# Gate's products for two token tiles at once: 256 columns instead of 128, and turned rows kept in pairs

## The chip, the core and the metric

The kernel runs on one core of a Trainium2 chip. The metric is the device time of one execution in microseconds. Before the change it is 1980.17 us, the median of 3 runs (1979.7 to 1982.45).

## What is computed

The reference is one transformer block: cross attention whose keys and queries both come from a context, then a mixture of eight experts beside one shared expert. Cut to what matters:

```python
# x: (4, 1024, 1024); four batches, 4096 tokens in all
x = x + attention(ctx) applied to layernorm(x)     # mixes the columns of each row
xt = layernorm(x).reshape(4096, 1024)
scores = sigmoid(xt @ gate_w.T)                    # gate_w: (8, 1024)
_, sel = top_k(scores + expert_bias, 2)
shared = silu(xt @ sw1.T) * (xt @ sw3.T) @ sw2.T   # the shared expert, float32
routed = grouped_swiglu(xt[tok] * score, w1, w2, w3)   # bfloat16, two experts a token
out = x + shared.at[tok].add(routed)
```

"Gate" below is the product `xt @ gate_w.T`: eight numbers for each token.

## The kernel before, in words

The tokens lie in 32 tiles of 128 rows (`NT`). A tile has 1024 columns, which are 8 blocks of 128 (`KC`); `HALF` is 4.

The work has four stages. The first, up to about 63 us, makes the attention of the first batch. The second takes the tiles in 16 pairs (loop over `p`, L583; `g = 2 * p` is the first tile). The third is the shared expert, in 8 blocks of 512 tokens (`up`, L913, and `down_pair`, L1009; the first block's `up` is `first_up`, L191, at the end of stage two). The fourth is the routed experts, in slots of 512 tokens (loop at L1125).

A pair of tiles of stage two consists of seven products of 512 columns (`product`, L399, through `seven`, L197; the matmuls are at L129). They are a 2 by 2 product in Strassen's manner, written out in seven terms. After each product comes a step `between(k)`, k from 0 to 6 (L619), which adds other work to TensorE's queue. This order is written by hand: in this stage TensorE, GpSimd, VectorE and ScalarE execute in the order of the program text, and only SP's queue (the loads and stores) is ordered by the framework's own scheduler. While three batches remain ahead (`ahead`, pairs 0 to 11), a pair also prepares two tiles of the next batch's attention: `energies` (L317), `softmax` (L326), `scaled` (L333), and `turned` (L342), which transposes the attention rows. In the last four pairs (12 to 15) nothing lies ahead, and these are left out.

The tiles touched by the change are these. A pair's sums, `x`, are normalised on ScalarE into `xt` (`second_norm`, L426). `turn` (L432) transposes the eight blocks of `xt` on TensorE into two PSUM tiles, `pt_t`, which ScalarE copies to `xtT` (L260). SP stores `xtT` to DRAM, `xtd` (L435), for the shared expert. `gate_parts` (L438) multiplies `xtT` by the gate's weights: eight matmuls of 128 columns in four groups of 32 array columns, each over two blocks, into the PSUM tile `gp` (L443); ScalarE copies it to `gs` (L446). `gate` (L449) adds the four groups with a small matmul with `sel`, into `lg` (L450). `route` (L452), `counts`, `lists_of` (L493), `weighted` (L513) and `scatter` (L523) then choose the experts and scatter the rows on VectorE, ScalarE and GpSimd.

The transposes of all kinds and `gp` share one pool of two PSUM buffers with the tag `pt` (`ps_t`, L115). `xtT` and `gs` have two SBUF buffers each, since pool `p2` (L231) has two by default.

In pairs 1 to 11 the order on TensorE is: turn of the previous pair's first tile; product 1; its gate; product 2; turn of the second tile; product 3; energies; product 4; gate of the second tile; `lg` of the first; transposes `pt_a` of `turned`; `lg` of the second; product 5, and so on. In pairs 12 to 15 it is: product 1; turn of the first; product 2; its gate; product 3; turn of the second; product 4; its gate; both `lg`; product 5. After the loop the last pair (tiles 30 and 31) is turned and gated among the first products of the shared expert, `pu` (L720 to L732).

The shared expert loads a block's turned rows with one DMA (`block`, L152) into `xb`, in which a row of 128 partitions has the axes tile, block of columns and token. `up` uses it as the moving operand, and GpSimd makes differences of its quarters, `xs` (L1109).

Of the kernel before, what the change touches and what calls it, by code (L numbers as in the profile page):

```python
# [31 lines left out]
F32 = mybir.dt.float32  # L32
# [8 lines left out]
P = 128  # L41
B, S, D = 4, 1024, 1024
C = 512
T = B * S
NT = T // P
HID = 704
E = 8
KC = D // P
# [6 lines left out]
G = 2  # L55
SLOT = 512
NQ = SLOT // P
# [20 lines left out]
def xattn_moe_kernel(ctx: ExitStack, tc: tile.TileContext, x, ctxT, wqT, wkT, bqk, gwT, ebias,  # L78
                     w13, w2, w2t, sw13, sw2, sw2t, consts, out):
    nc = tc.nc  # L80

    dram = ctx.enter_context(tc.tile_pool(name="dram", bufs=1, space=DRAM))
# [2 lines left out]
    w2tb = dram.tile([E * TAIL, D], BF16, name="w2tb")  # L85
    xrows = nc.dram_tensor("xrows", (E * T, ROW // 2), I32, kind="Internal").ap()
    x2d = dram.tile([T, D], F32, name="x2d")
    xtd = dram.tile([NT, P, D], F32, name="xtd")

    cp = ctx.enter_context(tc.tile_pool(name="cp", bufs=1))  # L90
    con = cp.tile([P, CONSTS], F32, name="con")
# [58 lines left out]
    cps, cur = [], {}  # L150

    def block(s):  # L152
        cur["xb"] = xb = cps[1].tile([P, NQ, KC, P], F32, tag="xb", name=f"xb_{s}")
        nc.sync.dma_start(xb.rearrange("p t c k -> p t (c k)"),
                          xtd[s * NQ : (s + 1) * NQ].rearrange("t p f -> p t f"))

    def of_two(ap):

# [68 lines left out]
    with ExitStack() as a:  # L227
# [22 lines left out]
        def transposed(dsts, src, n, second=None):  # L250

            for h, dst in enumerate(dsts):
                pt = ps_t.tile([P, HALF, P], F32, tag="pt", name=f"pt_{n}_{h}")
                for j in range(HALF):
                    c = h * HALF + j
                    nc.tensor.transpose(pt[:, j, :], src[:, c * P : (c + 1) * P], ident)  # L256
                if h and second:
                    nc.vector.tensor_copy(dst, pt)
                else:
                    nc.scalar.copy(dst, pt)  # L260
# [165 lines left out]
        def second_norm(g):  # L426
# [2 lines left out]
            xts[g] = xt = p2.tile([P, D], F32, tag="xt", name=f"xt_{g}", bufs=4)  # L429
            nc.scalar.activation(xt, x2, AF.Identity, bias=nb, scale=rs)  # L430

        def turn(g):  # L432
            xtT = p2.tile([P, KC, P], F32, tag="xtT", name=f"xtT_{g}")
            transposed([xtT[:, :HALF], xtT[:, HALF:]], xts[g], f"t{g}")
            nc.sync.dma_start(xtd[g], xtT.rearrange("p c t -> p (c t)"))  # L435
            return xtT

        def gate_parts(g, xtT):  # L438

            gp = ps_t.tile([P, P], F32, tag="pt", name=f"gp_{g}")  # L440
            for r in range(2):
                for j in range(4):
                    nc.tensor.matmul(gp[32 * j : 32 * (j + 1), :], gw_sb[:, 2 * j + r, :],  # L443
                                     xtT[:, 2 * j + r, :], start=r == 0, stop=r == 1)
            gs = p2.tile([P, P], F32, tag="gs", name=f"gs_{g}")
            nc.scalar.copy(gs, gp)  # L446
            return gs

        def gate(lg, g, gs):  # L449
            nc.tensor.matmul(lg[:, g % G, :], gs, sel, start=True, stop=True)  # L450

        def route(g, lg):  # L452

# [91 lines left out]
        with tc.manual_schedule(engines=vector_scalar):  # L545
# [33 lines left out]
            ps_a.close()  # L579
            ps_m, ps_e, ps_s = psum("ps_m", 1), psum("ps_e", 1), psum("ps_s", 1)  # L580

            routing, listing, xtTs, gss = {}, {}, {}, {}
            for p in range(NT // 2):  # L583
                g = 2 * p
                b, i = divmod(g, LT)
# [25 lines left out]
                    looked(i)  # L611
                if p:
                    if ahead:
                        xtTs[g - 2] = turn(g - 2)
                    second_norm(g - 1)
                if not new:
                    softened(i)
# [1 line left out]
                def between(k):  # L619
                    if k == 0:  # L620
                        if not ahead:
                            xtTs[g - 2] = turn(g - 2)
                        elif p:
                            gss[g - 2] = gate_parts(g - 2, xtTs.pop(g - 2))
                        if new:
                            next(halves)
                        if p > 1:
                            pc_, ss, ohs = listing[g - 4]
                            listing[g - 4] = lists_of(g - 4, pc_, ohs), ss
                        if g + 2 < NT:  # L630
                            load(g + 2)
                            load(g + 3)
                        if g == NT - LT:
                            nc.sync.dma_start(sw13_sb, sw13)
                    elif k == 1:
                        if new:
                            looked(i)
                            softened(i)
                        if not ahead:
                            gss[g - 2] = gate_parts(g - 2, xtTs.pop(g - 2))  # L640
                        elif p:
                            xtTs[g - 1] = turn(g - 1)
                        if ahead:
                            scaled(b + 1, i, on_scalar=True)
                        if p > 1:
                            tois, ss = listing.pop(g - 4)
                            listing[g - 4] = tois, [weighted(g - 4, j, ss) for j in range(G)]
                        if p in (1, 3, 5, 7, 10, 13):
                            convert((1, 3, 5, 7, 10, 13).index(p))
                    elif k == 2:  # L650
                        if not ahead:
                            xtTs[g - 1] = turn(g - 1)
                        looked(i + 1)
                        softened(i + 1)
                        if g + 2 < NT:
                            norms[g + 2] = statistics(xin[g + 2], f"1_{g + 2}")
                        if g + 2 == NT:
                            two_sums.close()
                            cps.append(pool(shared, "c3"))
                            block(0)  # L660
                    elif k == 3:
                        if p:
                            gss[g - 1] = gate_parts(g - 1, xtTs.pop(g - 1))
                            lg = ps_s.tile([P, G, E], F32, tag="lg", name=f"lg_{g}")
                            gate(lg, g - 2, gss.pop(g - 2))
                        if ahead:
                            turned(b + 1, i)
                            scaled(b + 1, i + 1, on_scalar=True)
                        if p:
                            gate(lg, g - 1, gss.pop(g - 1))  # L670
                            routing[g - 2] = route(g - 2, lg)
                        if p > 1:
                            scatter(g - 4, *listing.pop(g - 4))
                        if g + 2 < NT:
                            norms[g + 3] = statistics(xin[g + 3], f"1_{g + 3}")
                    elif k == 4:
                        if ahead:
                            turned(b + 1, i + 1)
                    elif k == 5:
                        if g + 2 < NT:  # L680
                            tokens(g + 2)
                        if p:
# [35 lines left out]
            v21, v22 = sw2_sb[:, KH : 2 * KH, :512], sw2_sb[:, KH : 2 * KH, 512:]  # L718
            ups = first_up(pool(a, "e1", 1, "right"))
            g = NT - 2  # L720
            xtT = turn(g)
            second_norm(g + 1)
            pc_, ss, ohs = listing.pop(g - 2)
            tois = lists_of(g - 2, pc_, ohs)
            next(ups)
            gs = gate_parts(g, xtT)
            xtT = turn(g + 1)
            scatter(g - 2, tois, [weighted(g - 2, j, ss) for j in range(G)])
            next(ups)
            lg = bank("lg_last")[:, : G * E].rearrange("p (g e) -> p g e", g=G)  # L730
            gate(lg, g, gs)
            gate(lg, g + 1, gate_parts(g + 1, xtT))  # L732
            nc.vector.tensor_tensor(ws[0], w21, w22, ALU.add)
            mask, ss, ohs = route(g, lg)
            next(ups)
# [172 lines left out]
    with shared, tc.manual_schedule(engines=vector_scalar | {mybir.EngineType.SP}):  # L908
# [4 lines left out]
        def up(s):  # L913
# [3 lines left out]
            for f in range(NF):  # L917
                if f == 1:
                    residuals(s)
                cols = slice(f * P, (f + 1) * P)  # L920
                a = [lambda c, w=w: w[:, c, cols] for w in (w11, w12, w22, *ws, w21)]
                b = [lambda c, x=x: x[:, :, c, :]
                     for x in (xb[:, :2, :HALF], xb[:, :2, HALF:], xb[:, 2:, HALF:], *cur["xs"])]
                pa, pb, pc_ = (bank(f"p{k}_{s}_{f}")[:, :256] for k in "abc")

                one, two, five = (c1.tile([P, 256], F32, tag=k, name=f"{k}_{s}_{f}", bufs=n)
# [151 lines left out]
        for s in range(NJ):  # L1078
# [25 lines left out]
            down_pair(s, 0)  # L1104
            if s + 1 < NJ:
                xb = cur["xb"]
                cur["xs"] = xs = [sx.tile([P, 2, HALF, P], F32, tag=f"xs{i}", name=f"xs{i}_{s}")
                                  for i in range(4)]
                differences(nc.gpsimd, xs[:3], xb[:, :2, :HALF], xb[:, 2:, :HALF], xb[:, :2, HALF:],  # L1109
                            xb[:, 2:, HALF:], xs[3], False)  # L1110
# [167 lines left out]
```

## Time and profile before

| what | us |
|---|---|
| median of 3 runs (range) | 1980.17 (1979.7 to 1982.45) |
| the profiled execution | 1977.36 |
| its span in the profile | 1975.6 |
| TensorE (PE) busy | 1940.2 |
| gate's matmuls (`gp<-xtT,gw_sb`), 512 records | 20.6 |
| transposes of `turn` (`pt_t`), 256 records | 33.5 |
| `lg` matmuls, 60 and 4 records | 10.6 for the 60 |
| granted TensorE clock | 0.997 |

The profile is of one execution; times in it count from the start of its span. PE is TensorE's matmuls and PEld its weight loads, which run beside them; DVE is VectorE, ACT ScalarE, POOL GpSimd, SP the queue of loads and stores. [...] The record of a matmul is longer than the distance to the next one, because matmuls are pipelined; distances between starts tell what TensorE spends. "a<-b,c" reads: tile a is written from b and c. An arrow after idle time names what ended it.

### The profile page before, as it was taken

The page shows a single profiled execution, that of the slowest core. Times are in us where ns is not written, and L with a number is a line of the kernel's source. Part 1 is how long each engine was busy: PE and PEld are TensorE (multiplying, and loading weights), DVE is VectorE, ACT ScalarE, POOL GpSimd, SP SyncE. Part 2 cuts the span into 40 slices and gives each one's busy share as a digit, 9 for nine tenths or more (in the row PEclk, how much of TensorE's full clock was granted, in tenths as well). Part 3 has the DMA queues.
Part 4 walks back from the last instruction along what each step waited for, and adds up shares of the span by engine and source line. Part 5 has one row for each costly group of instructions (what it writes and reads, how often), then busy time and mean ns, then how long its engine had stood idle before and what let it go on. Part 6 is the DMA issues. An engine that isn't in the chain of part 4 may idle for free.

```text
span 1975.6 us, 23759 instructions
## 1 busy us (share of the span) xinstructions
PE 1940.2 (98%) x8736; PEld 1157.9 (59%) x8851; DVE 809.3 (41%) x1981; ACT 514.4 (26%) x900; POOL 651.7 (33%) x598
## 2 busy tenths in 40 slices
PE   8999999999999999999999999999999999999997
PEld 5555655655444447676676758584845555446554
DVE  5456556555865324413232323223243333223343
ACT  3344454355434101010110101010102233223232
POOL 0424433543642140302222232213014454335454
PEclk9999999999999999999999999999999999999999
DMA  3277486447685216297776868586465598649995
GB/s 124 85 173 196 141 226 165 138 143 195 244 228 204 96 64 152 78 231 208 209 199 167 198 196 212 143 207 181 114 284 108 111 312 277 139 137 325 345 353 93
DMA packets 229394, 365.51 MB, mean 185 GB/s; under 512 B 114336, under 2 KB 170144, under 8 KB 222496
## 3 DMA queue, kind: packets, MB, share of 16 engines
q0 software_dynamic: 43024, 172.78, 33.0%
q1 hardware_dynamic: 186256, 191.21, 32.1%
q8 instruction: 71, 1.16, 0.2%
q14 instruction: 43, 0.35, 0.1%
HBM read 289.19 MB, written 174.59 MB: 235 GB/s over the span
## 4 chain that ended last, share of the span: by engine, by line
PE 91%; DMA 3%; DVE 2%; issue 1%; SPq 1%; POOL 1%; ACT 0%; POOLq 0%; DVEq 0%; ACTq 0%
PE pa L129 21%; PE bank L129 15%; PE pc L129 11%; PE bank L1150 7%; PE qa L129 6%; PE pb L129 5%; PE pu L129 4%; PE pq L308 3%; PE qc L129 3%; PE pe L320 3%; PE pt_c L129 2%; DMA xh<-xgt 2%; PE pt_a L256 1%; PE qb L129 1%; PE pt_t L256 1%; PE pt_x L256 1%
## 5 line engine op out<-in xcount | busy, mean ns | idle before, releaser
L129 PE MATMUL bank<-xTb,w 128*128 128x0 bf16 x2024 | 310.6, 315 | 3.1 <-issue 1.3
L129 PEld LDWEIGHTS <-w 128*128 128x128 bf16 x2024 | 189.2, 98 | 111.7 <-issue 1.0
L748 POOL DMA_INDIRECT xgt<-xrows,li x92 | 88.2, 959 | 439.8 <-DMA xh<-xgt 169.1
L1183 POOL DMA_INDIRECT out_dram<-yt,toks x92 | 148.3, 1611 | 137.4 <-DVE yt L1179 76.4
L1150 PE MATMUL bank<-w,hTb 128*128 128x0 bf16 x920 | 164.1, 326 | 0.0
L273 POOL TENSOR_TENSOR rs<-ve,con 128x1 f32<-128x1 f32 x64 | 47.8, 747 | 315.9 <-DVE ve L271 315.9
L146 DVE TENSOR_TENSOR hTb<-sg_b,bank 128x512 bf16<-128x512 f32 x115 | 78.8, 687 | 160.8 <-PE bank L129 159.0
L129 PE MATMUL pa<-xs,sw_sb 128*128 128x256 f32 x560 | 132.4, 380 | 0.3 <-DVE five L943 0.3
L1150 PEld LDWEIGHTS <-hTb 128*128 128x128 bf16 x920 | 72.2, 97 | 87.0 <-issue 11.4
L129 PE MATMUL pa<-aT,xT 128*128 128x512 f32 x256 | 116.8, 599 | 1.5 <-DVE x L410 1.4
L129 PEld LDWEIGHTS pa<-xs,sw_sb 128*128 128x128 f32 x560 | 106.5, 190 | 14.9 <-DVE five L943 0.7
L1179 DVE COPY yt<-bank 128x512 f32<-128x512 f32 x92 | 61.3, 689 | 122.6 <-PE bank L1150 120.5
L145 ACT ACTIVATE sg_b<-bank 128x512 f32<-128x512 f32 x115 | 68.5, 597 | 164.7 <-PE bank L129 160.5
L1181 ACT COPY yt<-bank 128x512 f32<-128x512 f32 x92 | 53.2, 587 | 144.5 <-PE bank L1150 137.6
L748 POOL DMA_INDIRECT w<-w13b,wi x23 | 22.9, 996 | 202.1 <-PE bank L129 149.5
L526 POOL DMA_INDIRECT xrows<-rr,toi x64 | 64.8, 1012 | 62.6 <-issue 39.6
L410 DVE SCALAR_TENSOR_TENSOR x<-pa,rs,x 128x512 f32<-128x512 f32 x64 | 47.9, 748 | 88.5 <-PE pa L129 82.6
L166 ACT ACTIVATE st_c<-pt_c 64x256 f32<-64x256 f32 x7 | 2.6, 378 | 311.4 <-PE pt_c L129 311.4
L266 DVE BATCH_NORM_STATS2 st<-x 128x6 f32<-128x512 f32 x128 | 81.8, 681 | 0.5
L1031 DVE TENSOR_TENSOR x2c<-x2c,qa 128x512 f32<-128x512 f32 x64 | 43.9, 685 | 92.9 <-PE qa L129 92.9
L129 PE MATMUL pu<-xb,sw_sb 128*128 128x512 f32 x176 | 76.3, 594 | 0.9 <-PE pt_t L256 0.9
L129 PEld LDWEIGHTS pa<-aT,xT 128*128 128x128 f32 x256 | 46.3, 191 | 48.8 <-issue 47.8
(262 smaller groups left out, 3322.8 us busy)
## 6 DMA issues: line engine op xcount, KB each, us to landing
xturned<-xh SPq DMA_DIRECT2D x46, 512.0 KB, 4.1
xTb<-xturned SPq DMA_DIRECT2D x23, 1024.0 KB, 6.2
w13b<-in_w_dram POOLq DMA_DIRECT2D x8, 2816.0 KB, 19.0
x<-in_x_dram SPq DMA_DIRECT2D x32, 512.0 KB, 4.1
x2d<-x SPq DMA_DIRECT2D x32, 512.0 KB, 4.9
xtd<-xtT SPq DMA_DIRECT2D x32, 512.0 KB, 4.5
xb<-xtd SPq DMA_DIRECT2D x8, 2048.0 KB, 10.0
x2c<-x2d SPq DMA_DIRECT2D x16, 1024.0 KB, 9.3
```

Source lines behind the costliest of these rows:

```text
L129: nc.tensor.matmul(part(pp), w(c), part(xT(c)), start=start and c == 0, stop=c == blocks - 1, skip_group_check=not start)
L145: nc.scalar.activation(sg, pa, AF.Silu)
L146: nc.vector.tensor_tensor(hT[:, f, :], sg, pb, ALU.mult)
L256: nc.tensor.transpose(pt[:, j, :], src[:, c * P : (c + 1) * P], ident)
L266: nc.vector.bn_stats(st[:, h, :], src[:, h * 512 : (h + 1) * 512])
L308: nc.tensor.matmul(pq[:, i, j, :], w[c // CH][:, c % CH, :], ct[c // CH][:, c % CH, :], start=c == 0, stop=c == CC - 1)
L320: nc.tensor.matmul(pe[:, h, :], qs[b][:, m * P : (m + 1) * P], ks[b][:, h * 512 : (h + 1) * 512], start=True, stop=True)
L526: nc.gpsimd.indirect_dma_start(out=places[2 * (g + i) + k], out_offset=bass.IndirectOffsetOnAxis(ap=tois[k][:, i : i + 1], axis=0), in_=rr ...
L748: nc.gpsimd.indirect_dma_start(out=dst, out_offset=None, in_=src, in_offset=bass.IndirectOffsetOnAxis(ap=idx, axis=0), **bound)
L1150: nc.tensor.matmul(part(py), hT[:, f, toks], part(w[:, f, cols]), start=False, stop=f == NF - 1, skip_group_check=q < 2)
L1179: nc.vector.tensor_copy(yt[:, q, h * 512 : (h + 1) * 512], py)
L1183: adds.append([nc.gpsimd.indirect_dma_start(out=outs[q], out_offset=bass.IndirectOffsetOnAxis(ap=toks[:, q : q + 1], axis=0), in_=yt[:, q, ...
```

## The change

`turn` now writes its tile into one half of the columns of a common tile of 256 tokens, a tile for each pair, with one buffer instead of two. When the second tile has been turned, one DMA stores the pair (1 MB). `gate_parts` runs once for a pair, on 256 columns, with one copy of 256 columns to `gs`, also in one buffer. `gate` issues both `lg` matmuls in a row.

In pairs 1 to 11 the gate after product 1 goes away and the one after product 4 is now for both tiles; both `lg` come after the transposes of `turned`. In pairs 12 to 15 the second tile is turned after product 2 instead of product 3, the gate comes after product 3, and both `lg` after product 4. In the last pair both turns come before the one gate. `xtd` and `xb` get the axes pair, block of columns, token (256), so a block's rows are loaded with 8 KB a run instead of 4 KB, and the shared expert's moving operand has 256 adjacent columns. In the queue of SP the first load of `xb` (tiles 0 to 3, issued in pair 15) now stands behind the store of tiles 28 and 29; before, it stood ahead of the store of tile 29.

```diff
-    xtd = dram.tile([NT, P, D], F32, name="xtd")
+    xtd = dram.tile([NT // 2, P, KC, 2 * P], F32, name="xtd")
...
+        xtTs = {}
+
         def turn(g):
-            xtT = p2.tile([P, KC, P], F32, tag="xtT", name=f"xtT_{g}")
-            transposed([xtT[:, :HALF], xtT[:, HALF:]], xts[g], f"t{g}")
-            nc.sync.dma_start(xtd[g], xtT.rearrange("p c t -> p (c t)"))
-            return xtT
-
-        def gate_parts(g, xtT):
-
-            gp = ps_t.tile([P, P], F32, tag="pt", name=f"gp_{g}")
+
+            if g % 2 == 0:
+                xtTs[g] = p2.tile([P, KC, 2 * P], F32, tag="xtT", name=f"xtT_{g}", bufs=1)
+            cols = slice(g % 2 * P, (g % 2 + 1) * P)
+            xtT = xtTs[g - g % 2]
+            transposed([xtT[:, :HALF, cols], xtT[:, HALF:, cols]], xts[g], f"t{g}")
+            if g % 2:
+                nc.sync.dma_start(xtd[g // 2], xtT)
+
+        def gate_parts(g):
+
+            xtT = xtTs.pop(g)
+            gp = ps_t.tile([P, 2 * P], F32, tag="pt", name=f"gp_{g}")
             for r in range(2):
                 for j in range(4):
                     nc.tensor.matmul(gp[32 * j : 32 * (j + 1), :], gw_sb[:, 2 * j + r, :],
                                      xtT[:, 2 * j + r, :], start=r == 0, stop=r == 1)
-            gs = p2.tile([P, P], F32, tag="gs", name=f"gs_{g}")
+            gs = p2.tile([P, 2 * P], F32, tag="gs", name=f"gs_{g}", bufs=1)
             nc.scalar.copy(gs, gp)
             return gs
 
-        def gate(lg, g, gs):
-            nc.tensor.matmul(lg[:, g % G, :], gs, sel, start=True, stop=True)
+        def gate(lg, gs):
+            for i in range(G):
+                nc.tensor.matmul(lg[:, i, :], gs[:, i * P : (i + 1) * P], sel, start=True, stop=True)
...
                     if k == 0:
                         if not ahead:
-                            xtTs[g - 2] = turn(g - 2)
-                        elif p:
-                            gss[g - 2] = gate_parts(g - 2, xtTs.pop(g - 2))
+                            turn(g - 2)
...
-                        if not ahead:
-                            gss[g - 2] = gate_parts(g - 2, xtTs.pop(g - 2))
-                        elif p:
-                            xtTs[g - 1] = turn(g - 1)
+                        if p:
+                            turn(g - 1)
...
                     elif k == 2:
                         if not ahead:
-                            xtTs[g - 1] = turn(g - 1)
+                            pair[g] = gate_parts(g - 2)
...
                     elif k == 3:
                         if p:
-                            gss[g - 1] = gate_parts(g - 1, xtTs.pop(g - 1))
+                            gs = gate_parts(g - 2) if ahead else pair.pop(g)
                             lg = ps_s.tile([P, G, E], F32, tag="lg", name=f"lg_{g}")
-                            gate(lg, g - 2, gss.pop(g - 2))
                         if ahead:
                             turned(b + 1, i)
                             scaled(b + 1, i + 1, on_scalar=True)
                         if p:
-                            gate(lg, g - 1, gss.pop(g - 1))
+                            gate(lg, gs)
                             routing[g - 2] = route(g - 2, lg)
...
             next(ups)
-            gs = gate_parts(g, xtT)
-            xtT = turn(g + 1)
+            turn(g + 1)
             scatter(g - 2, tois, [weighted(g - 2, j, ss) for j in range(G)])
             next(ups)
             lg = bank("lg_last")[:, : G * E].rearrange("p (g e) -> p g e", g=G)
-            gate(lg, g, gs)
-            gate(lg, g + 1, gate_parts(g + 1, xtT))
+            gate(lg, gate_parts(g))
...
-                b = [lambda c, x=x: x[:, :, c, :]
-                     for x in (xb[:, :2, :HALF], xb[:, :2, HALF:], xb[:, 2:, HALF:], *cur["xs"])]
+                b = [lambda c, x=x: x[:, c, :]
+                     for x in (xb[:, 0, :HALF], xb[:, 0, HALF:], xb[:, 1, HALF:], *cur["xs"])]
```

More of the change, by code (lines that the diff above doesn't have):

```diff
@@ L152, in block @@
     def block(s):
-        cur["xb"] = xb = cps[1].tile([P, NQ, KC, P], F32, tag="xb", name=f"xb_{s}")
-        nc.sync.dma_start(xb.rearrange("p t c k -> p t (c k)"),
-                          xtd[s * NQ : (s + 1) * NQ].rearrange("t p f -> p t f"))
+        cur["xb"] = xb = cps[1].tile([P, 2, KC, 2 * P], F32, tag="xb", name=f"xb_{s}")
+        nc.sync.dma_start(xb.rearrange("p u c k -> p u (c k)"),
+                          xtd[2 * s : 2 * (s + 1)].rearrange("u p c k -> p u (c k)"))
     def of_two(ap):
@@ L580, in xattn_moe_kernel @@
             ps_m, ps_e, ps_s = psum("ps_m", 1), psum("ps_e", 1), psum("ps_s", 1)
-            routing, listing, xtTs, gss = {}, {}, {}, {}
+            routing, listing, pair = {}, {}, {}
             for p in range(NT // 2):
@@ L621, in between @@
                         if not ahead:
-                            xtTs[g - 2] = turn(g - 2)
-                        elif p:
-                            gss[g - 2] = gate_parts(g - 2, xtTs.pop(g - 2))
+                            turn(g - 2)
                         if new:
@@ L720, in xattn_moe_kernel @@
             g = NT - 2
-            xtT = turn(g)
+            turn(g)
             second_norm(g + 1)
@@ L1106, in xattn_moe_kernel @@
                 xb = cur["xb"]
-                cur["xs"] = xs = [sx.tile([P, 2, HALF, P], F32, tag=f"xs{i}", name=f"xs{i}_{s}")
+                cur["xs"] = xs = [sx.tile([P, HALF, 2 * P], F32, tag=f"xs{i}", name=f"xs{i}_{s}")
                                   for i in range(4)]
-                differences(nc.gpsimd, xs[:3], xb[:, :2, :HALF], xb[:, 2:, :HALF], xb[:, :2, HALF:],
-                            xb[:, 2:, HALF:], xs[3], False)
+                differences(nc.gpsimd, xs[:3], xb[:, 0, :HALF], xb[:, 1, :HALF], xb[:, 0, HALF:],
+                            xb[:, 1, HALF:], xs[3], False)
             if s == 0:
```

## The prediction

> **What bounds the kernel now.** I read the page first: busy shares, slices, then the shares of the chain that ended last.
>
> ```profile
> PE 1940.2 (98%) x8736; PEld 1157.9 (59%) x8851; DVE 809.3 (41%) x1981; ACT 514.4 (26%) x900; POOL 651.7 (33%) x598
> PE   8999999999999999999999999999999999999997
> PE 91%; DMA 3%; DVE 2%; issue 1%; SPq 1%; POOL 1%; ACT 0%; POOLq 0%; DVEq 0%; ACTq 0%
> ```
>
> TensorE is full in all slices and carries the chain. So I asked for busy time by stretch; one pair of token tiles of the second stage (94.8 to 129.6 us) answers:
>
> ```profile
> 94.80:129.60 34.80, 34.80 (x151) 18.30 (x150) 17.55 (x49) 15.82 (x26) 9.95 (x15) 1.00 0.89 212
> ```
>
> The columns are length, then PE, PEld, DVE, ACT and POOL busy: PE 34.80 of 34.80 us. Nothing hides a microsecond of TensorE here; taking one away shortens the kernel unless another engine becomes late. Next, what gate costs in that stream. The weight loads in order of time show it (start, length):
>
> ```profile
> 98.26 0.19 PEld L129 LDWEIGHTS pa<-aT,xT 128*128 128x128 f32 x1 [0.24 <-issue]
> 99.21 0.38 PEld L443 LDWEIGHTS gp<-xtT,gw_sb 128*32 128x32 f32 x16 [0.76 <-ACT at L329]
> 99.78 0.30 PEld L129 LDWEIGHTS pc<-t,s 128*128 128x128 f32 x2 [0.20 <-issue]
> 100.32 0.19 PEld L129 LDWEIGHTS pc<-t,s 128*128 128x128 f32 x1 [0.24 <-issue]
> ...
> 111.92 0.19 PEld L129 LDWEIGHTS pb<-aT,xT 128*128 128x128 f32 x1 [0.24 <-issue]
> 112.87 0.38 PEld L443 LDWEIGHTS gp<-xtT,gw_sb 128*32 128x32 f32 x16 [0.76 <-issue]
> 113.44 0.30 PEld L450 LDWEIGHTS lg<-sel,gs 128*128 128x128 f32 x2 [0.20 <-issue]
> 113.58 0.94 PEld L256 LDWEIGHTS pt_a<-con,at 128*128 128x128 f32 x8
> 114.49 0.30 PEld L450 LDWEIGHTS lg<-sel,gs 128*128 128x128 f32 x2
> 114.71 0.30 PEld L129 LDWEIGHTS pa<-aT,xT 128*128 128x128 f32 x2
> 115.26 0.19 PEld L129 LDWEIGHTS pa<-aT,xT 128*128 128x128 f32 x1 [0.24 <-issue]
> ```
>
> Loads of 512-column products are 0.43 us apart. From the load at 98.26 to the fourth at 100.32 are three steps, 1.29 without gate: this gate costs 2.06 - 1.29 = 0.77. The second: from 111.92 to 115.26 is 3.34; the same kind of stretch without gate (117.40 to 119.56) takes 2.16; so gate and its two small lg products cost 1.18 (gate 0.67, first lg 0.28, second 0.23).
>
> **Gate's products.** A gate is 16 records, four column groups side by side, so four waves. Waves follow at 0.11 us: the pace of streaming 128 columns (eight transposes take 0.87 us, 0.109 each; eight 256-column records 1.73, 0.216; eight of 512 3.44, 0.43). Streaming costs exactly double at double width, so the four waves get no cheaper: 4 x 0.107 = 0.43 for each tile either way. What one gate for two tiles saves is one set of edges, 0.77 - 0.43 = 0.34 per pair. A gate of 256 costs 0.77 + 0.43 = 1.20 between products.
>
> **Pairs 1 to 11** (an attention batch is prepared beside them). Removed: 0.77 after the first product and 1.18 in the fourth step, 1.95. Added in the fourth step: a gate, 1.12 (an estimate: its last edge is some 0.08 smaller ahead of transposes); both lg after the transposes, four loads of about 0.11 in a row, 0.37 to 0.46, I take 0.41; and a new wait. The transposes pt_a use the two PSUM buffers that gate's output uses too, so the second four wait for ScalarE's copy gs, which no other work on TensorE stands in for (lg used to). The trace has the copy at both widths:
>
> ```profile
> L446 ACT COPY gs<-gp 128x128 f32<-128x128 f32 x32 | 8.5, 266 | 65.8 <-PE gp L443 65.8
> L938 ACT COPY two<-pa 128x256 f32<-128x256 f32 x35 | 13.0, 372 | 49.6 <-PE pa L129 49.6
> ```
>
> The copy starts 0.14 after the next instruction on TensorE begins (99.92 against 99.78), takes 0.37, and TensorE follows 0.05 later: 0.56. Four transposes hide 0.44 + 0.02. The wait is 0.10, and about 0.06 for a load no longer ahead: 0.16; bounds 0 (the copy is seen sooner) and 0.56 (nothing hidden). [...] Queued behind the waiting transposes are lg and the next product; behind the copy on ScalarE the aT copies, 0.1 later, due only at the fifth step's transposes. After: 1.12 + 0.41 + 0.16 = 1.69. Saved 0.26, x 11 = 2.8 us (1.1 to 4.5).
>
> **Pairs 12 to 15.** Here the fourth step has no transposes, and the second lg waits for gs: from the load at 613.57 to that at 616.36 is 2.79 against 1.29, so 1.50; with the other gate 0.77, 2.27. Turning the second tile moves one step forward, to where its xt has been ready for 4 us (602.0 against 606.0); gate moves to the third step (1.20), and gs is done a product before lg (0.41). After 1.61, saved 0.66. In pair 12 it is worth nothing: the fifth product waits for VectorE (idle 1.4 before pa in the waits), whose copies rr take 4.34 and 4.37 us there instead of 0.75 and 0.18, beside GpSimd's two long differences, and none of that moves. Three pairs: 2.0 us (1.7 to 2.7 if pair 12 gains after all).
>
> **The last pair.** The chain in order of time:
>
> ```profile
> 629.65 7.12 PE pu L129 x16
> ...
> 638.90 0.37 ACT sv_c L168
> 639.27 0.03 issue
> 639.29 0.28 ACT gs L446
> 639.57 0.04 issue
> 639.61 0.66 PE pt_t L256 x4
> ```
>
> Turning tile 31 waits for tile 30's gs, which stands behind a table load and three operations on ScalarE. After the change no gate lies between the turns: 636.77 to 640.27 (3.5) becomes the bare transposes (0.87), 2.6 saved. Later one gate of 256, its exposed copy (0.11 longer) and two lg take 2.2 where 1.6 stood. Net 2.0 (1.4 to 2.2). VectorE and ScalarE have 13.7 us of pu ahead of them before the six banks come round, so I see nothing late next.
>
> **What costs nothing.** ScalarE's 32 copies of 0.27 become 16 of 0.37; its stretch is 15.8 busy of 34.8. SP issues 16 stores instead of 32. Store order: a half stays until its partner is turned, some 8 us; but xtd is read by the eight xb loads alone. The first xb load now queues on SP behind the store of tiles 28 and 29: issued near 610 instead of 603.7, landing within the 12.3 us maximum, 622, and first used at 629.65. The x loads keep their places ahead of the stores. The new order of xb's columns: two runs of 128 (L129 on xb) take 379 ns, one run of 256 (wk's projection) 379, so neither products nor GpSimd's differences (2.34 us a piece) change.
>
> **One xtT tile instead of two.** The next pair's first copy waits until the store of the last has landed. The trace:
>
> ```profile
> L435 SPq DMA_DIRECT2D xtd<-xtT x32: 319/320/431, 96.8 to 640.9; - x32
> ...
> DMA to landing us min/median/max: 2.6/4.5/9.2
> ```
>
> 512 KB land within 9.2 us at worst, so 1 MB within 18.4. The store is issued at about 104.3 and the next copy due at 130.2: 25.9 us (19 at the last pair). [...] I take zero.
>
> **Sum.** 2.8 + 2.0 + 2.0 = 6.8 us. The profiled execution took 1977.36 (span 1975.6 and 1.8 around it): 1970.6. It stands 2.8 below the median of the runs, 1980.17, which gives 1973.4.
>
> **Rivals.**
> 1. The gain is hidden: gs comes late behind ScalarE's exponentials so that the 0.56 is open in all 11 pairs (-1.6), and other waits take the tail back; 2.0 is left: 1978. For it: two buffers shared by three users. Against: ScalarE is idle 1.6 us before gs at 113.58. 0.18.
> 2. Everything fits: no copy wait (4.5), pair 12 too (2.7), tail 2.2: 9.4, so 1970.8. 0.14.
> 3. Slower: the single tile. The price is the excess of a store's landing over 25.9 us, 15 times; it turns the sum from 26.4 us on (0.45 x 15 = 6.8). [...] For it: stores share the DMA engines with the weight conversions, which land after 24.5 us in this stretch. Against: under them xtd still landed in 8.7. 0.06.
> 4. As computed: 1973.4, own range 1971 to 1975. 0.62.
>
> A measurement of this kernel tells about 0.2%, 4 us. Rivals 2 and 4 are faster, rival 1 is the same: 0.76, 0.18, 0.06. The range from 1970 to 1978 leaves out rival 3 and the far ends of 1 and 2.
>
> **What would show it.** Right: L443's successor has 256 records of some 380 ns; a pair of 34.8 becomes 34.5; pt_a waits about 0.1 us for gs eleven times; the wait of pt_t for gs in the tail (1.7 in the waits) is gone. Wrong: xtT copies waiting for a DMA; waves farther apart than 0.22 us, which would mean the column groups no longer run side by side; a pair at 34.8.

## The result and the profile after

The changed kernel takes 1973.16 us, the median of 6 runs (1969.79 to 1973.84), where the kernel before, run beside it, takes 1979.93 (6 runs, 1976.89 to 1982.45). The ratio is 0.9964, interval 0.9952 to 0.9976: 6.8 us faster, where 6.8 was predicted. (An interval here is the 95% interval of the ratio.)

The page of the changed kernel, busy shares, slices and chain, answers to the first three lines shown of before:

```profile
PE 1940.1 (98%) x8480; PEld 1155.5 (59%) x8595; DVE 810.4 (41%) x1981; ACT 512.9 (26%) x884; POOL 653.0 (33%) x598
PE   8999999999999999999999999999999999999997
PE 89%; DMA 5%; SPq 2%; DVE 2%; issue 1%; ACT 0%; POOL 0%; POOLq 0%; DVEq 0%; ACTq 0%
```

There are 256 fewer records of matmuls and 16 fewer copies on ScalarE, and TensorE's busy time has hardly moved (1940.2 to 1940.1). That is no contradiction: a record is longer than the distance to the next (379 ns for 256 columns, where waves follow at 0.216 us), and the groups of gate's rows say what became of them (durations are least, median and greatest in ns, then first and last start in us):

```profile
L450 PE MATMUL gp<-xtT,gw_sb x256: 379/379/403, 114.6 to 650.4; 128*32 128x256 f32 x128
L453 ACT COPY gs<-gp x16: 372/372/373, 115.8 to 650.8; 128x256 f32<-128x256 f32 x16
L442 SPq DMA_DIRECT2D xtd<-xtT x16: 319/320/384, 106.8 to 638.8; - x16
```

Half as many records (a gate's eight matmuls leave 16), of 379 ns where they took 273; half as many copies, of 372 where they took 266; half as many stores: the change does what it says. The same pair as was shown of before, in the same columns:

```profile
97.34:131.92 34.58, 34.58 (x136) 18.01 (x135) 17.56 (x49) 15.74 (x25) 9.97 (x15) 1.00 0.87 210
```

34.80 has become 34.58, and TensorE is busy in all of it: the gain in a pair is 0.22. The weight loads of its fourth step are:

```profile
113.69 0.19 PEld L129 LDWEIGHTS pb<-aT,xT 128*128 128x128 f32 x1 [0.24 <-issue]
114.63 0.59 PEld L450 LDWEIGHTS gp<-xtT,gw_sb 128*32 128x32 f32 x16 [0.76 <-issue]
115.63 0.98 PEld L256 LDWEIGHTS pt_a<-con,at 128*128 128x128 f32 x8 [0.41 <-issue]
116.58 0.53 PEld L458 LDWEIGHTS lg<-sel,gs 128*128 128x128 f32 x4
117.03 0.30 PEld L129 LDWEIGHTS pa<-aT,xT 128*128 128x128 f32 x2
117.57 0.19 PEld L129 LDWEIGHTS pa<-aT,xT 128*128 128x128 f32 x1 [0.24 <-issue]
```

From 113.69 to 117.57 are 3.88, and without gate 2.16: the step now holds 1.72 of gate and `lg`, and there is no other gate in the pair. In the last pair the chain of waits no longer has ScalarE between the two turns:

```profile
628.02 7.11 PE pu L129 x16
635.13 0.87 PE pt_t L256 x8
636.00 13.73 PE pu L129 x32
649.74 1.04 PE gp L450 x16
...
650.81 0.38 ACT gs L453
...
651.23 0.61 PE lg_last L458 x4
```

The second turn is a bare 0.87 where 3.50 stood. Later one gate, one copy and four `lg` take 2.10 (649.74 to 651.84) where 1.47 stood.

To compare kernels by stage I use distances between starts of the same matmul of the same pair. These are single executions. Pair 0 is left out, since no gate stands in it; "stage two" in comparisons below is the row "stage two from pair 1 on":

| us | before | after |
|---|---|---|
| ten pairs, fourth product of pair 1 to that of pair 11 | 375.58 | 373.50 |
| start of pair 1 (its first turn) to the last product of pair 11 | 404.27 | 401.97 |
| from there through pair 12 | 34.10 | 34.13 |
| pairs 13 to 15 | 89.67 | 87.77 |
| the last pair, beside `pu` | 80.83 | 78.83 |
| stage two from pair 1 on | 615.68 | 609.51 |
| stage three | 726.49 | 725.27 |
| from it to stage four | 38.41 | 40.02 |
| stage four | 500.21 | 499.84 |

(A row of `pu`'s first 6.8 us is left out; it is the same in both.) Stage two gained 6.17: 2.30 in pairs 1 to 11, nothing in pair 12, 1.90 in the next three, 2.00 in the last. The two profiled executions differ only by 3.5 (1977.36 and 1973.84), because in the one after pair 1 began 2.5 later (97.34 against 94.81) and the passage to stage four took 1.6 more. Neither belongs to the change; both are looked at in the last section. Nor can the 1.2 of stage three be laid to it: in the 13 traces that stage takes from 723.7 to 728.3, and with the new layout alone (experiment 3) it takes 726.62.

### The profile page after: what moved, and what is told of

It reads as the page before. It is cut to its first block, busy times and chain, and to the rows that moved or that the text cites. A ratio compares the mean times of both kernels' runs of the same rounds, so it can differ in the third digit from the quotient of the medians.

```text
span 1972.0 us, 23197 instructions
## 1 busy us (share of the span) xinstructions
PE 1940.1 (98%) x8480; PEld 1155.5 (59%) x8595; DVE 810.4 (41%) x1981; ACT 512.9 (26%) x884; POOL 653.0 (33%) x598
## 3 DMA queue, kind: packets, MB, share of 16 engines
q8 instruction: 69, 1.13, 0.2%
## 4 chain that ended last, share of the span: by engine, by line
PE 89%; DMA 5%; SPq 2%; DVE 2%; issue 1%; ACT 0%; POOL 0%; POOLq 0%; DVEq 0%; ACTq 0%
PE pa L129 19%; PE bank L129 15%; PE pc L129 10%; PE bank L1151 8%; PE qa L129 6%; PE pb L129 5%; DMA xh<-xgt 4%; PE pu L129 4%; PE pq L308 3%; PE pe L320 3%; PE qc L129 3%; PE pt_c L129 2%; PE pt_a L256 2%; SPq L1004 2%; PE qb L129 1%; PE pt_t L256 1%
## 5 line engine op out<-in xcount | busy, mean ns | idle before, releaser
L941 DVE TENSOR_TENSOR one<-one,pb 128x256 f32<-128x256 f32 x35 | 14.7, 421 | 149.4 <-PE pb L129 140.1
```

## The experiments

**1. The gate of 256 as two of 128, back to back.** The edges and the width are taken apart: the records are again 512 of 128 columns, but between products there is one gate a pair.

```diff
-            for r in range(2):
-                for j in range(4):
-                    nc.tensor.matmul(gp[32 * j : 32 * (j + 1), :], gw_sb[:, 2 * j + r, :],
-                                     xtT[:, 2 * j + r, :], start=r == 0, stop=r == 1)
+            for i in range(2):
+                own = slice(i * P, (i + 1) * P)
+                for r in range(2):
+                    for j in range(4):
+                        nc.tensor.matmul(gp[32 * j : 32 * (j + 1), own], gw_sb[:, 2 * j + r, :],
+                                         xtT[:, 2 * j + r, own], start=r == 0, stop=r == 1)
```

> The changed kernel, but the one gate of 256 columns is written as two gates of 128 columns right behind each other into the two halves of the same PSUM tile: the order, the copy and everything else stay. Theory (what was saved is one gate's edges of 0.34 us; streaming costs the same at any width): eight waves of 0.107 us in place of four of 0.216, the gate lasts as long as the wide one within 0.1 us, so the time is that of the changed kernel, 1973, within 1.5 us. Rival (each record has a fixed cost, and the saving came from 256 fewer records, 6.8 us / 256 = 27 ns each): the time is back at the kernel before, 1980, and each gate is 0.4 us longer.

Measured: 1973.61 (9 runs), ratio to before 0.9964, interval 0.9951 to 0.9977. The records are 273 ns again:

```profile
L452 PE MATMUL gp<-xtT,gw_sb x512: 272/273/297, 113.2 to 650.6; 128*32 128x128 f32 x171
```

The 32 records of a pair take 1.01 from first start to the next instruction, the 16 of the changed kernel 1.00; ten pairs take 373.85 against 373.50. So 256 columns at a time instead of 128 are worth 0.01 of the gain of 0.22 in the gate itself and 0.03 a pair in all. What gained in these pairs was that the two gates stand together, and products and gates follow each other half as often. (The trace's pair 12 takes 35.25, 1.1 more, for a stretch at half the clock that the last section shows.)

**2. Each gate issued twice.** It puts a price on what is left of gate, and tests whether TensorE's time in this place is the kernel's time.

```diff
-            for r in range(2):
+            for r in range(4):
...
-                    nc.tensor.matmul(gp[32 * j : 32 * (j + 1), :], gw_sb[:, 2 * j + r, :],
-                                     xtT[:, 2 * j + r, :], start=r == 0, stop=r == 1)
+                    nc.tensor.matmul(gp[32 * j : 32 * (j + 1), :], gw_sb[:, 2 * j + r % 2, :],
+                                     xtT[:, 2 * j + r % 2, :], start=r % 2 == 0, stop=r % 2 == 1)
```

> The changed kernel with each gate's eight matmuls issued twice (the second set overwrites the first with the same numbers). Theory: no new edges, four more waves of 0.216 us, so 0.86 us for each of 16 gates, 13.8 us in all, less what the stall in pair 12 and the exposed copies take up: 12.5 to 13.8 us over the changed kernel, about 1986.5. Rival (a gate's time is mostly fixed, and its width hardly counts): under 5 us. Rival (the four column groups don't really run side by side): 16 more records of 0.216 us a gate, 3.4 us each, 55 us in all.

Measured: 1983.94 (10 runs), ratio to before 1.0017, interval 1.0006 to 1.0028, so 10.8 above the changed kernel's 1973.16. In its trace the ten pairs take 8.55 more (0.855 each, four waves of 0.216 being 0.86), pair 12 nothing (34.11), the three after it 2.60, the last pair 0.86. The price of a wave is paid in full wherever TensorE is dense, and in pair 12 it is not paid at all. The whole, 12.8 in stage two, is within what was expected; the medians, taken from other executions, show 10.8, under the expected 12.5.

**3. The new layout in DRAM and in `xb`, nothing else,** on the kernel before.

```diff
-    xtd = dram.tile([NT, P, D], F32, name="xtd")
+    xtd = dram.tile([NT // 2, P, KC, 2 * P], F32, name="xtd")
...
-            nc.sync.dma_start(xtd[g], xtT.rearrange("p c t -> p (c t)"))
+            nc.sync.dma_start(xtd[g // 2][:, :, g % 2 * P : (g % 2 + 1) * P], xtT)
...
-                     for x in (xb[:, :2, :HALF], xb[:, :2, HALF:], xb[:, 2:, HALF:], *cur["xs"])]
+                     for x in (xb[:, 0, :HALF], xb[:, 0, HALF:], xb[:, 1, HALF:], *cur["xs"])]
```

> The kernel before, with only the storage changed: xtd and xb in the order pair, block, 256 tokens, stores of one tile in runs of 512 bytes into it, and the shared expert reading 256 adjacent columns; gate stays as before. Theory: 0 us, the shared expert's stage (first qa to the last pa<-xs) takes 726.5 us as before, and stage two is unchanged because the stores are hidden. Rival (a part of the gain is from the adjacent columns in the third stage, which took 725.3 us in the changed kernel): the stage gets 1 us shorter here too, and the kernel is about 1 us faster.

Measured: 1979.12 (10 runs), ratio 0.9991, interval 0.9978 to 1.0004. Ten pairs take 375.58 as before, stage three 726.62 against 726.49. The layout is worth nothing that these runs can tell.

**4. A version for each of the waits that I saw left:** gate a product earlier in pairs 1 to 11, so that products lie between the copy `gs` and the transposes; in the last pair `lg` a product after gate; and in pair 12 the copies `rr` moved from the step after product 2 to the step after product 4.

```diff
-                        if p > 1:
+                        if p > 1 and g != NT - LT:
...
-                        if not ahead:
+                        if p:
                             pair[g] = gate_parts(g - 2)
...
-                            gs = gate_parts(g - 2) if ahead else pair.pop(g)
+                            gs = pair.pop(g)
...
+                        if g == NT - LT:
+                            tois, ss = listing.pop(g - 4)
+                            listing[g - 4] = tois, [weighted(g - 4, j, ss) for j in range(G)]
...
-            lg = bank("lg_last")[:, : G * E].rearrange("p (g e) -> p g e", g=G)
-            gate(lg, gate_parts(g))
+            gs = gate_parts(g)
...
+            next(ups)
+            lg = bank("lg_last")[:, : G * E].rearrange("p (g e) -> p g e", g=G)
+            gate(lg, gs)
```

> The changed kernel with three more moves of order. (a) In pairs 1 to 11 the gate stands after product 3, ahead of the energies, as in the last four pairs, so the copy gs is done long before the transposes need its PSUM buffer. (b) In pair 12 the copies rr of the rows to be scattered move from the second step to the fourth, behind the addition of product 4, so that GpSimd's long differences don't hold up VectorE ahead of the additions that TensorE waits for. (c) In the last pair, gate stands one step of the shared expert before lg. Theory: (a) 0.08 us a pair, 0.9 us in all, and no wait of pt_a; (b) the wait of pa for VectorE in pair 12 (2.0 us in the changed kernel) goes, 1.5 to 2.3 us; (c) the wait of lg_last for gs goes, 0.6 us. Together 3.0 to 3.8 us under the changed kernel, about 1969.7. Rival (other waits stand right behind these: GpSimd's differences themselves, the scatter): under 1.5 us.

Measured: 1974.09 (8 runs), ratio to before 0.9972, interval 0.9959 to 0.9985: not below the changed kernel, and the expectation is missed. In its trace two parts are as expected, ten pairs 372.64 (0.86 less) and the last pair 78.26 (0.57 less). Pair 12, where the most was to come, took 35.22, and pairs 13 to 15 took 89.26, 1.5 more, with the clock at half from 531.2 to 534.7. Experiments 7, 9 and 10 look for the reason in pair 12.

**5. The last pair's order alone,** on the kernel before: both turns, and later both gates and all `lg`.

```diff
-            gs = gate_parts(g, xtT)
-            xtT = turn(g + 1)
+            xtT1 = turn(g + 1)
...
-            gate(lg, g, gs)
-            gate(lg, g + 1, gate_parts(g + 1, xtT))
+            gs = [gate_parts(g, xtT), gate_parts(g + 1, xtT1)]
+            for i in range(G):
+                gate(lg, g + i, gs[i])
```

> The kernel before, with only the last pair's order changed: tile 31 is turned right after tile 30's tails, and both gates, still of 128 columns, come behind the next step. Theory: the wait of pt_t for gs (1.7 us in the waits of before) goes and the rest of that stretch stays about the same, so from the first product pu to the fourth step's counts the kernel takes 1.8 to 2.3 us less than before; the time falls by about 2 us. Rival (the wait only moves, to lg_last or to the banks of pu): under 0.7 us.

Measured, in a single execution: 1976.62, one of before beside it 1983.59. Ten pairs take 375.59, pairs 13 to 15 89.68, as before; the last pair 78.51 against 80.83. That is 2.3 by the order alone, with narrow gates; the changed kernel, with the wide gate in this place, has 78.83. So the gain of the last pair is this order's. (Pair 12 took 35.18 here, again with a stretch at half the clock, so stage two is 614.44.)

**6. Every pair stored twice,** the second time to a DRAM tile that nobody reads, so that the one `xtT` buffer comes free later.

```diff
+                nc.sync.dma_start(xtd2[g // 2], xtT)
```

> The changed kernel, which also stores each pair's turned rows a second time, to a place that nobody reads. Both stores have to land before the one xtT tile is written again. Theory: the two land within 20 us and there are 25.9, so stage two takes as long as in the changed kernel within 0.5 us, and no ScalarE copy xtT waits for a DMA. Rival (the single buffer is at its limit): copies xtT wait for the store, and stage two grows by several us, up to 15 landings more.

Measured, in a single execution: 1976.05; ten pairs 373.87 against 373.50. What `xtT`'s engines waited for, and how long the stores took (ACT's copies `xtT` are among the instructions counted):

```profile
L444 SPq DMA_DIRECT2D xtd<-xtT x16: 424/432/1426, 105.3 to 639.2; - x16
its engine sat idle before it (us, times) until:
  PE pt_t L257: 59.1, 18
  issue: 9.9, 13
  ACT rr L526: 2.3, 3
...
DMA to landing us min/median/max: 3.9/7.3/16.1
```

No DMA stands in the list of what ended the waits. The longest landing that the trace has is 16.1; from a store to the next copy are 19.6 to 30.9 in this trace, though twice the bytes go out. The other half of the expectation is missed: stage two takes 611.47, 2.0 more than in the changed kernel. Of this 1.1 is a stretch at half the clock in pair 12, and about 0.45 a matmul of pair 8 that waits for a load, `ct`, from DRAM; the 0.48 in pairs 13 to 15 was not followed up. None of it is a wait for the `xtT` buffer. A second `xtT` buffer was not tried.

**7. Only `rr` moved in pair 12,** the first and the fourth edit of experiment 4 without the rest.

> The changed kernel with (b) of the combined kernel alone: in pair 12 the copies rr move from the second step to the fourth. Theory: the two rr pieces that took over 4 us each beside GpSimd's differences fall outside them, the addition of product 3 is on time, and the stall of pa in pair 12 (2.0 us) goes; 1.5 to 2.3 us gained from product 1 of pair 12 to product 1 of pair 13. Rival (GpSimd's differences hold up the pair in any case, through the scatter or rs): under 0.7 us.

Measured, in a single execution: 1972.52, and pair 12 at 34.96, no less than 34.13: the expectation is missed. VectorE's order of time (start, length; idle before) shows why. First the changed kernel:

```profile
514.57 4.37 DVE L525 TENSOR_SCALAR rr<-xt,ss 128x1024 bf16<-128x1024 f32 x1
518.97 4.37 DVE L526 CAST rr<-con 128x32 int32<-128x32 f32 x1
...
524.12 0.74 DVE L410 SCALAR_TENSOR_TENSOR x<-pa,rs,x 128x512 f32<-128x512 f32 x1
```

and then this experiment:

```profile
515.47 0.75 DVE L410 SCALAR_TENSOR_TENSOR x<-pa,rs,x 128x512 f32<-128x512 f32 x1 [3.39 <-PE pa L129]
521.00 1.29 DVE L266 BATCH_NORM_STATS2 st<-x 128x6 f32<-128x512 f32 x2 [4.78 <-DMA x<-in_x_dram]
...
523.43 0.74 DVE L525 TENSOR_SCALAR rr<-xt,ss 128x1024 bf16<-128x1024 f32 x1
524.21 0.18 DVE L526 CAST rr<-con 128x32 int32<-128x32 f32 x1
```

`rr` is 0.74 and 0.18 away from GpSimd's differences, as expected, and the sum of `pa` comes at 515.47 where it came at 524.12 (2.5 of this is that the whole execution runs earlier). But then the statistics of the next tile stand for 4.78 until its rows have been loaded from DRAM, at 521.0. That load waits for the stores `x2d`, which were issued behind 5.6 MB of the shared expert's weights. The waits of PE and of SP in this stretch, and the DMA issues from 490 to 522 (size of one, median us to landing), show the chain. A line of waits has the us in total, the times and the longest:

```profile
SPq L376 <- DMA x2d<-x: 3.9, 2, 3.0
```

```profile
sw_sb<-in_sw_dram SPq DMA_DIRECT2D x1, 5632.0 KB, 19.1
x2d<-x SPq DMA_DIRECT2D x2, 512.0 KB, 17.6
...
x<-in_x_dram SPq DMA_DIRECT2D x2, 512.0 KB, 4.9
```

```profile
PE pa L129 <- DVE x L410: 3.4, 1, 3.4
```

The weights are issued at 496.07 (L640), the stores behind them take 17.6 to land, the load of x is issued at 516.1, when they have, and lands 4.9 later. What VectorE does after it comes little earlier than it did, and product 7 pays 3.4 in place of the 2.0 that product 5 paid.

**8. The early gate and the last pair of experiment 4, without moving `rr`.**

> The changed kernel with (a) and (c) of the combined kernel: the gate after product 3 in all pairs, and apart from lg in the last pair. Theory: a pair of 34.58 us becomes 34.50, pt_a waits for nothing, lg_last waits for nothing; 0.9 + 0.6 = 1.5 us less in stage two. Rival (the copy gs, now behind ScalarE's rr pieces, comes late and holds up the exponentials and with them the transposes): no gain or a loss.

Measured, in a single execution: 1966.59. Ten pairs 372.64, pair 12 34.12, last pair 78.27: stage two 607.99, 1.52 below the changed kernel, as expected. Experiment 11 takes its time over several runs.

**9. Experiment 4 with the 5.6 MB loaded in four pieces,** one in each of pairs 12 to 15.

```diff
-                        if g == NT - LT:
-                            nc.sync.dma_start(sw13_sb, sw13)
+                        if g >= NT - LT:
+                            own = slice(p % 4 * 2, p % 4 * 2 + 2)
+                            nc.sync.dma_start(sw13_sb[:, own], sw13[:, own])
```

> The combined kernel (early gate, rr later in pair 12, gate apart from lg at the end), with the shared expert's first weights, 5.6 MB, loaded in four pieces over pairs 12 to 15 instead of at once in pair 12. Theory (in pair 12 three things stood one behind the other: rr beside GpSimd's differences, then the load of x behind the 5.6 MB, which ended at 520.9 and held up VectorE's statistics and with them rs): with both gone pair 12, 34.1 us in the changed kernel, takes under 32.0, and without the long idle of TensorE there is no half-clock stretch of 3.4 us in it either; the kernel takes 1966 or less. Rival (GpSimd's own differences, 10 us, and the scatter behind them hold pair 12): over 33.3 us.

Measured: 1970.45 (6 runs), before beside it 1978.57, ratio 0.9959, interval 0.9943 to 0.9975. VectorE in pair 12:

```profile
515.28 0.75 DVE L410 SCALAR_TENSOR_TENSOR x<-pa,rs,x 128x512 f32<-128x512 f32 x1 [3.39 <-PE pa L129]
515.95 1.28 DVE L266 BATCH_NORM_STATS2 st<-x 128x6 f32<-128x512 f32 x2
```

The statistics follow the sum at once; the wait for the load is gone, and pair 12 takes 32.30, 1.8 less than 34.12. The expectation (under 32.0, no stretch at half the clock in pair 12, and a kernel of 1966 or less) is met in its second part alone.

**10. The four pieces alone,** on the changed kernel, with `rr` where it was.

> The changed kernel with the load of 5.6 MB in four pieces, and nothing else. Theory (rr stands ahead of the load's wait): the wait of pa for VectorE in pair 12 stays near 2 us, since the rr pieces still take over 4 us; pair 12 gains under 0.8 us. Rival (the load of x was the cause of the whole stall, and rr only seemed to be): pair 12 gains 2 us.

Measured, in a single execution: 1971.98, pair 12 34.13, ten pairs 373.51. Splitting the load alone gains nothing, moving `rr` alone loses 0.8, both together gain 1.8 (one trace each): the two waits stand one behind the other, and each hides the other.

**11. Experiment 8 again, timed,** beside experiment 9 on one chip.

> The same kernel as the early gate one, timed. Theory: 1.5 us under the changed kernel's 1973.2 in stage two, so about 1971.7, and in the trace a stage two of 608 us again; the 1966.59 of the single run was below that because it had no half-clock stretch and a quick start. Rival (the early gate gains far more, 6 us): 1967.

Measured: 1971.46 (7 runs, 1967.91 to 1975.79), ratio to before 0.9961, interval 0.9948 to 0.9975. The single 1966.59 was a lucky execution. In the traces stage two is 1.5 shorter than the changed kernel's in both executions (607.99 and 608.01), but by their ratios the changed kernel (0.9964), this one and experiment 9 (0.9959) can't be told apart. Nor do the traces tell this one from experiment 9: there stage two takes 607.86, because the 1.8 gained in pair 12 was given back in the last pair (79.95 against 78.27), where the clock was at half from 623.4 to 626.8. Without that stretch it would be about 606.2, an estimate from these numbers that no run shows.

## Why the prediction was right, point by point

- **TensorE's time is the kernel's time in this stage.** Right: four added waves of 0.216, which are 0.86, come back as 0.855 a pair (experiment 2).
- **Width saves nothing, edges do.** Right. Issued as two gates of 128 next to each other, the same kernel takes 1.01 for the gate instead of 1.00, and its time can't be told from the changed kernel's (experiment 1). The gate's own part is shown by the two orders of time on TensorE, before and after:

```profile
112.87 0.65 PE L443 MATMUL gp<-xtT,gw_sb 128*32 128x128 f32 x16
113.45 0.39 PE L450 MATMUL lg<-sel,gs 128*128 128x8 f32 x2
113.69 1.07 PE L256 MATMUL pt_a<-con,at 128*128 128x128 f32 x8
114.60 0.29 PE L450 MATMUL lg<-sel,gs 128*128 128x8 f32 x2
114.74 1.11 PE L129 MATMUL pa<-aT,xT 128*128 128x512 f32 x2
```

```profile
114.64 1.07 PE L450 MATMUL gp<-xtT,gw_sb 128*32 128x256 f32 x16
115.64 1.22 PE L256 MATMUL pt_a<-con,at 128*128 128x128 f32 x8
116.69 0.51 PE L458 MATMUL lg<-sel,gs 128*128 128x8 f32 x4
117.06 1.10 PE L129 MATMUL pa<-aT,xT 128*128 128x512 f32 x2
```

- **Pairs 1 to 11: 2.8 predicted, 2.3 measured.** Read start to start: gate grew from 0.58 to 1.00 (0.42, where 0.45 was counted); the transposes from 0.91 to 1.05; the four `lg` from 0.24 and 0.14 to 0.37. The `lg` are the term that was mis-sized: putting them together was counted at 0.10 saved and gave 0.01. The wait of `pt_a` for `gs` was rightly counted at 0.16 in all; 0.14 to 0.18 is measured, by whether the old 0.91 or eight transposes alone (0.87) are taken off (its 0.06 for a load was the author's estimate, and no run shows it by itself). So the step grew by 0.55 and not by 0.51, the other gate's 0.77 goes, and 0.21 to 0.22 a pair is left of 0.26.
- **The new wait.** It is there in all eleven pairs (1.05 to 1.06, once 1.13), near the value taken and far from the 0.56 of rival 1. Most of it can't be seen among the trace's waits, since a transpose's record reaches over it; distances show it. Taking it away by moving gate a product earlier gave 0.086 a pair (experiment 8), not 0.16: the gate then has products of 512 columns on both sides, and its last edge comes back (the energies behind it take 1.82 between starts instead of 1.72).
- **Pairs 13 to 15: 2.0 predicted, 1.9 measured** (89.67 to 87.77). Between starts, the gates of a pair go from twice 0.57 to 1.00, and the `lg`, which no longer wait for `gs`, from 0.75 to 0.37. So 0.38 of the 0.63 a pair comes from the order; the order alone was not run in these pairs.
- **Pair 12: nothing predicted, nothing measured.** The stall of the fifth product grew to take in what was saved, from 1.4 to 2.0:

```profile
PE pa L129 <- DVE x L410: 2.0, 1, 2.0
```

 But the reason given, VectorE's `rr` beside GpSimd (4.37 us each beside the differences, 0.74 and 0.18 away from them), was half of it. With `rr` out of the way a load of x, kept back by stores that take 17.6 to land behind 5.6 MB, holds the same pair as long (experiments 7, 9, 10).
- **Last pair: 2.0 predicted, 2.0 measured,** 2.63 saved and 0.63 given back, as forecast; the order alone gives 2.3 (experiment 5).
- **At no cost: layout, stores, one buffer, SP's order.** Right as far as runs go: the layout by experiment 3, the one buffer by experiment 6, SP's order by the first `pu`, which waits 0.86 in both kernels. The 25.9 was read at one pair: in the changed kernel 20.1 to 30.9 lie between a store and the next copy. With landings of at most 16.1 at twice the bytes, rival 3's price is still never met: no wait for a landing is there that a second `xtT` buffer could take away.
- **The sum.** 6.8 predicted, 6.8 in the medians, 6.2 in the traces' stage two. The two agree within what the medians can tell: the interval of the ratio is 4.8 us wide. That the medians meet the forecast to 0.2 us is luck, since the terms miss by 0.5 and 0.1. And about half of the 6.2 (2.0 in the last pair, 3 x 0.38 in pairs 13 to 15) is the new order's and not the joined gate's.

## What to carry to other kernels

Where TensorE is dense, cost a batch of small matmuls by its streamed columns (here 0.109 us a wave of 128 and 0.216 a wave of 256) and by how often it is entered and left among other shapes (here 0.77 for a gate between products, whose four waves make 0.44); joining two calls saves one entry, and whether the columns become wider records or stay at 128 hardly mattered here. Where a stall has a named releaser, ask what the releaser would wait for next before you count the gain: in pair 12 neither of two cures gained anything alone, and together they gained 1.8 us. And when two users of a small pool come next to each other, count the copy between them less the work that covers it, from distances between starts and not from the list of waits.

## What the runs showed of the hardware

In some traces TensorE's distances double for 3.4 us after a stop. The same place in pair 12, behind the same stall, in the changed kernel and in experiment 1 (length, busy times, the granted clock third from the end):

```profile
525.00:529.00 4.00, 3.99 (x10) 1.85 (x11) 3.69 (x15) 0.00 (x0) 1.77 (x3) 1.00 0.01 2
```

```profile
524.50:529.00 4.50, 4.50 (x8) 1.88 (x7) 4.05 (x19) 0.00 (x0) 2.53 (x4) 0.62 0.12 46
```

Both stood idle for 2.0 us before. In one the clock is whole. In the other it is 0.62 over the stretch, being at half for 3.4 us of it, and the pair takes 35.25 instead of 34.13. In the changed kernel's profiled execution this happened at the passage to stage four's chain near 1434, where `qa` and `qc` took 2.47 and 2.90 after an idle 2.04, while before they took 1.96 and 1.72 after 2.13:

```profile
1432.50 2.04 issue
1434.55 2.47 PE qa L129 x4
1437.02 2.90 PE qc L129 x4
1439.92 0.86 PE qd L1022 x2
```

The clock is at half from 1435.9 to 1439.3 there, and 512-column records follow at 0.854 instead of 0.429. That is the 1.6 of the table's "from it to stage four". Ahead of stage four, 9 of the 13 traces have one or two such stretches, all with the clock at half for 3.4 us, at a cost of 1.1 to 1.9 us each. The passage to stage four shows it best: it takes 39.9 to 40.1 in the seven traces that have one there, and 38.2 to 38.4 in the six that have none. All stand just behind a stop of TensorE: 1.4 in pair 12 of experiment 5, 1.2 and 0.9 close together ahead of the first `pu` in experiments 3 and 9, and 1.9 to 3.6 in the others. None stands in the dense pairs. The same stops pass in other traces without one, even 3.4 in pair 12 of experiment 7; what sets one off is not shown. How much of the 4 to 11 us by which runs of one kernel differ comes from such stretches is not shown, since only one execution of each has a trace.

Ahead of the late start of pair 1 distances are doubled too. At the start of the kernel 256-column matmuls follow at 0.427 us, until 7.4 us in the execution before and until 12.4 in the one after, and at 0.216 from then on. The trace's entries of the clock begin only there, whole, at 7.7 and at 12.5, so what it was before is not shown. First after, then before:

```profile
8.58 3.62 PE L308 MATMUL pq<-ct,wk_sb 128*128 128x256 f32 x8
```

```profile
7.99 1.89 PE L308 MATMUL pq<-ct,wk_sb 128*128 128x256 f32 x8
```
